# A ninth buffer for half operands in a recurrence, paid for with two shorter rings

## The chip, the cores and the metric

The kernel runs on one core of a Trainium2 chip. The metric is the device time of one execution in microseconds (us), as a median over repeated runs. The core has the engines TensorE (PE in the profile; its weight loads are PEld), VectorE (DVE), ScalarE (ACT), GpSimd (POOL) and SyncE (SP). All of them share 16 DMA engines for transfers between the on-chip memory and DRAM. Transfers issued from SP run on one hardware queue (q1 in the profile), those issued from POOL on a software queue (q0).

## The reference, cut to what matters

The program is one pass of a network with a two-dimensional LSTM, an attention layer and a feed-forward layer that contains a recurrence over time. Only that last recurrence is touched. For 16 images of 4096 tokens with 128 features:

```python
Wx = jnp.einsum('bti,hi->bth', x, W)
Wx = ((flat - mean) * rsqrt(var + eps) * gamma + beta)     # over all B*T rows
Vt = V.T
def step(yt, wx_t):
    yt = jax.nn.sigmoid(wx_t + yt @ Vt)
    return (yt, yt)
_, ys = jax.lax.scan(step, y0, jnp.swapaxes(Wx, 0, 1))      # 4096 steps in order
t = t + swapaxes(ys, 0, 1)
```

## The kernel before

Three stages follow each other: the LSTM, the attention layer for all images, and the recurrence (function `recurrence`, from L1494). The attention stage leaves the products Wx in DRAM (`wx`) and has already written x plus its own result into the output. The recurrence adds its states to that output.

**How the recurrence is tiled.** The 4096 tokens of an image are cut into 128 chunks of 32 (`STEPS`), which are run side by side: each chunk starts from zero, takes 12 warm-up steps (`WARM`) over the last tokens of the chunk before it, and then its own 32 steps (44 in all, `ALL`). A check at the end compares the warmed-up starts with the true ends. Two images (`GI`) form a pair, called a group in the code, and a state `rc_y` of a pair is a tile of 128 features by 2 x 128 columns (1 KB per partition). There are 8 pairs. Four of them are live at a time (`LANES`); the pairs of the first round start at steps 0, 5, 10 and 15 of the common loop, those of the second round at 45, 50, 55 and 60 (`starts`, L1617). The loop has 105 steps.

**One step** of a live pair: PE multiplies the last state by V (`product`, L1587) into PSUM; DVE adds the scaled operand (`state`, L1600); ACT applies the sigmoid (L1608). Every second step of a pair, `turn` (L1569) transposes its two newest states on PE (L1577), and ACT copies the result into a tile `rc_tt` (L1578) that holds four steps (4 KB per partition). When a tile `rc_tt` is full, which takes two such copies two steps apart, POOL issues a DMA that adds it into the output in DRAM (L1581); the DMA reads 512 KB of states and accumulates. So a pair makes 8 such tiles, and the whole recurrence 64. POOL has eight completion semaphores in turn for these DMAs: a store waits for the one eight before it.

**Where the operands lie.** The operand of a pair is cut into two halves by time (`h`): half 1 holds the upper 16 of the 32 tokens of every chunk, half 0 the lower 16. Half 1 is used first (warm-up), from the pair's first step, then half 0 from step 12 to 27, then half 1 again from step 28 to 43. A half takes 16 KB per partition and is loaded by four DMAs from SP of 512 KB each (`load`, L1557, and `half_image`, L1486). There are eight rooms for halves, tags `w0` to `w7`. Rooms 0 to 3 hold the halves of the first two pairs and are loaded during the attention stage (`ahead`, L1748). Rooms 4 to 7 are loaded at the beginning of the recurrence. In the second round the pair in lane l takes over the two rooms of the pair that ran in lane l before: its half 1 goes where the other pair's half 0 was, and its half 0 where the other's half 1 was.

**What sets the order.** PE, DVE, ACT and POOL run in the order in which the loop writes the instructions, with a manual schedule around it. The dictionary `due` (L1618) gives the step at which each load is written into SP's queue. It sets only the order on that queue: SP issues a load as soon as the room's last reader is done and a completion semaphore is free.

**The rings.** States `rc_y` come from a ring of 24 tiles, tiles `rc_tt` from a ring of 10. A tile is reused when its last reader is done; for `rc_tt` that is the DMA of L1581.

Of the kernel before, what the change touches and what calls it, by code (L numbers as in the profile page):

```python
# [8 lines left out]
F32 = mybir.dt.float32  # L9
# [6 lines left out]
P = 128  # L16
# [3 lines left out]
HALF = STEPS // 2  # L20
# [7 lines left out]
def idle_products(nc, out, ident, w, *sizes):  # L28

    for n in sizes:  # L30
        nc.tensor.matmul(out[:, :n], ident, w[:, :n], start=True, stop=True)
# [1462 lines left out]
def recurrence(nc, tc, wx, wx_stats, t2, v, gamma, beta, ident, mhalf, out, early, filler):  # L1494

    B, H = wx.shape[:2]
    N = t2.shape[1]
    L = STEPS
    CH = N // L
    C = 16
    G = CH // C
    S = 4
    NB = L // S
    GI = 2
    LANES = 4  # L1510
    WARM = 12
    AGREE = 2.0 ** -18
    NG = B // GI
    ALL = WARM + L
    APART = 5
    with ExitStack() as ctx:
        cp = ctx.enter_context(tc.tile_pool(name="rc_c", bufs=1))
        vT = cp.tile([P, P], F32, name="rc_vT")
        scale = cp.tile([P, 1], F32, name="rc_scale")
        shift = cp.tile([P, 1], F32, name="rc_shift")  # L1520
        res = cp.tile([P, NG], F32, name="rc_res")
        with ExitStack() as fast:
            wp = fast.enter_context(tc.tile_pool(name="rc_wp", bufs=1))
            yp_ = fast.enter_context(tc.tile_pool(name="rc_yp", bufs=1))
            tp = fast.enter_context(tc.tile_pool(name="rc_tp", bufs=10))
            ps_z = fast.enter_context(tc.tile_pool(name="rc_psz", bufs=4, space=PSUM))
            ps_t = fast.enter_context(tc.tile_pool(name="rc_pst", bufs=4, space=PSUM))

            def fill(*sizes):
                if sizes:  # L1530
                    idle_products(nc, ps_t.tile([P, 512], F32, tag="t", name="rc_t"), ident, filler, *sizes)


            vp = ps_t.tile([P, 4, P], F32, tag="t", name="rc_t")
            nc.tensor.transpose(vp[:, 0, :], v, ident)
            nc.scalar.copy(vT, vp[:, 0, :])
            nc.scalar.activation(shift, mhalf[:, 0:1], AF.Sigmoid)
            fill(*[384] * 8)
            mv = cp.tile([P, 2], F32, name="rc_mv")
            nc.vector.bn_aggr(mv, wx_stats.rearrange("p c s -> p (c s)"))  # L1540
            inv_std(nc, cp, scale, mv[:, 1:2], mhalf, "rc")
            nc.vector.tensor_mul(scale, scale, gamma)
            nc.vector.tensor_mul(shift, mv[:, 0:1], scale)
            nc.vector.tensor_sub(shift, beta, shift)

            class Group:
                pass

            def place(g):
                gr = Group()  # L1550
                gr.g = g
                gr.images = slice(g * GI, (g + 1) * GI)
                gr.w, gr.ys = {}, {}
                gr.last = None
                return gr

            def load(gr, h, n):  # L1557

                k = 2 * (gr.g % LANES) + (1 - h if gr.g < LANES else h)
                if gr.g < LANES and k in early:  # L1560
                    gr.w[h] = early["w", k]
                    return
                if n == 0:
                    pool = early.get(k, wp)
                    gr.w[h] = pool.tile([P, GI, G, HALF, C], F32, tag=f"w{k}", name=f"rc_w{k}")
                i, k = divmod(n, 2)
                half_image(nc, wx, gr.w[h], gr.g * GI + i, h, i, k)

            def turn(gr, s):  # L1569

                k, r = divmod(s, S)
                if r == 0:
                    gr.tt = tp.tile([P, GI, S, H], F32, tag="tt", name="rc_tt")
                yp = ps_t.tile([P, GI, 2, P], F32, tag="t", name="rc_t")
                for i in range(GI):
                    for j in range(2):
                        nc.tensor.transpose(yp[:, i, j, :], gr.ys[s + j][:, i, :], ident)  # L1577
                nc.scalar.copy(gr.tt[:, :, r : r + 2, :], yp)  # L1578
                if r == S - 2:
                    rows = out[gr.images].rearrange("b (c l) f -> c b l f", l=L)[:, :, k * S : (k + 1) * S, :]  # L1580
                    nc.gpsimd.dma_start(out=rows, in_=gr.tt, accum_op=ALU.add)  # L1581

            def product(gr):
                gr.z = None
                if gr.last is not None:
                    gr.z = ps_z.tile([P, GI, CH], F32, tag="z", name="rc_z")
                    nc.tensor.matmul(gr.z, vT, gr.last, start=True, stop=True)  # L1587

            def state(gr, n):


                s = (n - WARM) % L
                w = gr.w[s // HALF][:, :, :, s % HALF, :]
                y = yp_.tile([P, GI, CH], F32, tag="y", name="rc_y", bufs=24)
                yg = y.rearrange("p i (g c) -> p i g c", c=C)
                gr.last = y
                if gr.z is None:
                    nc.scalar.activation(yg, w, AF.Sigmoid, bias=shift, scale=scale)
                    return
                nc.vector.scalar_tensor_tensor(  # L1600
                    yg, w, scale, gr.z.rearrange("p i (g c) -> p i g c", c=C), ALU.mult, ALU.add
                )
                if n == WARM - 1:
                    gr.last = gr.y0 = yp_.tile([P, GI, CH], F32, tag="y0", name="rc_y0", bufs=LANES)
                    nc.vector.memset(gr.y0[:, :, 0:1], 0.0)
                    nc.scalar.activation(gr.y0[:, :, 1:CH], y[:, :, 0 : CH - 1], AF.Sigmoid, bias=shift)
                    return
                nc.scalar.activation(y, y, AF.Sigmoid, bias=shift)  # L1608
                gr.ys[n - WARM] = y

            def check(gr):
                d = yp_.tile([P, GI, CH - 1], F32, tag="d", name="rc_d")
                nc.vector.tensor_sub(d, gr.y0[:, :, 1:CH], gr.last[:, :, 0 : CH - 1])
                nc.vector.tensor_reduce(res[:, gr.g : gr.g + 1], d, AX.XY, ALU.max, apply_absolute_value=True)


            starts = [APART * (g % LANES) + (ALL + 1) * (g // LANES) for g in range(NG)]  # L1617
            due = {  # L1618
                (g, h, n): 0 if g < LANES else starts[g] - (10 if h else 0) + n
                for h in (1, 0) for g in range(NG) for n in range(2 * GI)  # L1620
            }
            groups = {g: place(g) for g in range(NG)}
            with tc.manual_schedule(
                engines={mybir.EngineType.PE, mybir.EngineType.DVE, mybir.EngineType.Activation, mybir.EngineType.Pool}
            ):
                for t in range(max(starts) + ALL + 1):
                    for (g, h, n), at in due.items():
                        if at == t:
                            load(groups[g], h, n)
                    live = [(groups[g], t - starts[g]) for g in range(NG) if 0 <= t - starts[g] <= ALL]  # L1630
                    for gr, n in live:
                        if n < ALL:
                            product(gr)
                    fill(*{1: (384, 256), 2: (384,), 3: (128,)}.get(len(live), ()))
                    for gr, n in live:
                        if n < ALL:
                            state(gr, n)
                    for gr, n in live:
                        s = n - WARM
                        if s > 0 and s % 2 == 0:  # L1640
                            turn(gr, s - 2)
                        if n == ALL:
                            check(gr)

        worst = cp.tile([P, 1], F32, name="rc_worst")
        nc.vector.tensor_reduce(worst, res, AX.X, ALU.max)
        nc.gpsimd.partition_all_reduce(worst, worst, P, bass_isa.ReduceOp.max)
        flag = cp.tile([P, 1], mybir.dt.int32, name="rc_flag")
        nc.vector.tensor_scalar(flag, worst, AGREE, None, ALU.is_gt)
        again = nc.values_load(flag[0:1, 0:1], min_val=0, max_val=1)  # L1650
        with tc.If(again != 0):
            in_order(nc, tc, wx, t2, vT, scale, shift, ident, out)
# [165 lines left out]
```

## Time and profile before

| what | us |
|---|---|
| three runs | 3641.32, 3644.18, 3649.93 (median 3644.18) |
| the profiled execution's own time | 3651.45 |
| its span, first to last instruction | 3649.9 |
| first state of the recurrence (ACT, L1598) | at 3388.16 |
| first store of states issued (POOL, L1581) | at 3420.18 |
| last store issued | at 3639.17 |

Mean busy time of the engines over the whole span: PE 96%, DVE 82%, ACT 68%, POOL 68%. The mean hides the stages. By windows of the recurrence:

| window, us | PE busy | ACT busy | DMA share | granted PE clock |
|---|---|---|---|---|
| 3440 to 3482 (42) | 42.00 | 41.76 | 1.08 | 1.00 |
| 3482 to 3520 (38) | 28.31 | 25.62 | 1.09 | 0.91 |
| 3520 to 3548 (28) | 27.16 | 27.07 | 1.09 | 1.00 |
| 3548 to 3612 (64) | 64.00 | 63.85 | 1.13 | 1.00 |

"DMA share" is the share of time in which the 16 DMA engines had packets under way; about 1 means that they never rest. A line of the waits reads: engine, tile and line that waited, then whom it waited for, then the sum, the number of waits and the longest. A wait for several semaphores is put down to the one that came last by the profile; where the engine named had long been done, it was another, often a DMA. "Landing" is the time from the issue of a DMA to its completion.

### The profile page before, as it was taken

What the parts mean: (1) busy time and instruction counts of PE and PEld (TensorE: products, weight loads), DVE (VectorE), ACT (ScalarE), POOL (GpSimd) and SP (SyncE); (2) the same over time, 40 slices, a digit from 0 to 9 for tenths busy, and PEclk for the clock granted to TensorE, in tenths of its full rate; (3) what the DMA queues carried; (4) which work ended last, traced back from release to release, by engine and by line L of the source; (5) the groups of instructions that cost most, each with busy time, mean ns of one, the idle gap of its engine ahead of it and who ended that gap; (6) DMA issues with size and microseconds to landing.
All of it is one profiled execution on the core that took longest, in us unless ns stands there. A gap on an engine that the chain in (4) does not pass through costs nothing. (4 is left out here: it accounts for less than half of the span.)

```text
span 3649.9 us, 99050 instructions
## 1 busy us (share of the span) xinstructions
PE 3499.9 (96%) x36874; PEld 2368.8 (65%) x36874; DVE 2991.3 (82%) x6997; ACT 2498.5 (68%) x5126; POOL 2484.0 (68%) x3840
## 2 busy tenths in 40 slices
PE   6899999999999998999999999999999999997988
PEld 5666665545567666975666666666666666654777
DVE  7799999998889887534888888888888888888665
ACT  0466566656667665345788888888888888876787
POOL 1577877777788885324777777777777777775123
PEclk9999999999999999999999999999999999999999
DMA  9223232333333221023677666776767677657799
GB/s 320 102 76 80 80 85 80 81 85 84 88 87 85 80 77 35 4 61 96 147 187 188 162 161 161 166 166 161 163 162 165 165 164 165 156 140 189 196 274 183
DMA packets 834182, 484.04 MB, mean 133 GB/s; under 512 B 304672, under 2 KB 800672, under 8 KB 833696
## 3 DMA queue, kind: packets, MB, share of 16 engines
q1 hardware_dynamic: 811034, 441.36, 47.3%
q0 software_dynamic: 17728, 34.61, 5.2%
q8 instruction: 294, 4.82, 0.6%
q10 hardware_dynamic: 4934, 1.68, 0.2%
q14 instruction: 192, 1.57, 0.2%
HBM read 239.21 MB, written 238.29 MB: 131 GB/s over the span
## 5 line engine op out<-in xcount | busy, mean ns | idle before, releaser
L1081 POOL TENSOR_TENSOR at_total<-at_total,at_e 128x512 f32<-128x512 f32 x472 | 601.5, 1274 | 238.4 <-ACT at_e L1054 218.8
L274 ACT ACTIVATE ls_g<-ls_z,ls_b 128x304 f32<-128x304 f32 (+26 forms) x950 | 492.8, 545 | 220.1 <-PE ls_z L272 189.0
L267 PE MATMUL ls_z<-ls_xn,ls_w 128*128 128x432 f32 (+28 forms) x1700 | 586.1, 492 | 1.5 <-POOL ls_xn L259 1.2
L267 PEld LDWEIGHTS ls_z<-ls_xn,ls_w 128*128 128x128 f32 x1700 | 309.4, 190 | 189.0 <-issue 97.8
L272 PE MATMUL ls_z<-ls_hsum,ls_u 128*128 128x304 f32 (+26 forms) x1140 | 366.8, 458 | 0.0
L1013 DVE TENSOR_REDUCE at_mxq<-at_bank 128x1 f32<-128x512 f32 x512 | 317.8, 683 | 55.2 <-PE at_bank L1009 54.9
L307 POOL TENSOR_TENSOR ls_tt<-ls_ve,mhalf 128x8 f32<-128x8 f32 (+2 forms) x190 | 313.0, 1647 | 19.8 <-DVE ls_ve L306 4.2
L1158 ACT ACTIVATE at_eT<-at_bank 128x512 f32<-128x512 f32 x512 | 264.3, 603 | 42.0 <-PE at_bank L1153 41.4
L272 PEld LDWEIGHTS ls_z<-ls_hsum,ls_u 128*128 128x128 f32 x1140 | 208.9, 191 | 128.6 <-issue 78.2
L390 ACT ACTIVATE ls_g<-ls_cell 128x304 f32<-128x304 f32 (+26 forms) x190 | 93.2, 491 | 267.2 <-DVE ls_cell L389 267.1
L272 PE MATMUL ls_z<-ls_h,ls_u 128*128 128x304 f32 (+26 forms) x760 | 254.9, 458 | 11.9 <-DVE ls_h L394 11.9
L324 ACT ACTIVATE ls_tt<-ls_tt,ls_nb 128x128 f32<-128x128 f32 (+9 forms) x632 | 261.0, 478 | 5.5 <-POOL ls_tt L307 5.0
L386 POOL TENSOR_TENSOR ls_g<-ls_g,ls_cell 128x304 f32<-128x304 f32 (+26 forms) x190 | 180.3, 949 | 123.6 <-ACT ls_g L274 110.7
L1124 DVE TENSOR_REDUCE at_cmx<-at_bank 128x8 f32<-128x512 f32 x256 | 175.6, 686 | 103.5 <-PE at_pair L1116 102.0
L259 POOL TENSOR_TENSOR ls_xn<-ls_xn,grstd 128x272 f32<-128x272 f32 (+40 forms) x186 | 209.4, 1126 | 73.6 <-DVE ls_xn L254 70.5
L1229 ACT COPY at_fx<-at_bank 128x512 f32<-128x512 f32 x128 | 133.5, 1043 | 142.3 <-PE at_bank L1225 137.8
L1600 DVE SCALAR_TENSOR_TENSOR rc_y<-rc_w,rc_scale,rc_z 128x256 f32<-128x256 f32 x344 | 154.6, 481 | 86.0 <-PE rc_z L1587 84.2
L1219 ACT ACTIVATE at_z<-at_u,at_nb,at_r 128x128 f32<-128x128 f32 x512 | 209.5, 484 | 4.7 <-POOL at_nb L1214 4.5
L272 PEld LDWEIGHTS ls_z<-ls_h,ls_u 128*128 128x128 f32 x760 | 140.5, 190 | 106.5 <-issue 52.6
L1581 POOL DMA_DIRECT2D out_dram<-rc_tt x64 | 77.4, 1209 | 168.0 <-ACT rc_tt L1578 142.2
L1174 DVE STREAM_TRANSPOSE at_t<-at_bank 128x512 f32<-128x512 f32 x256 | 167.9, 695 | 28.6 <-PE at_bank L1165 27.7
L1587 PE MATMUL rc_z<-rc_y,rc_vT 128*128 128x256 f32 x688 | 173.0, 391 | 12.3 <-ACT rc_y L1608 11.6
(279 smaller groups left out, 9806.1 us busy)
## 6 DMA issues: line engine op xcount, KB each, us to landing
at_win<-vd SPq DMA_DIRECT2D x256, 256.0 KB
t<-ls_tt SPq DMA_DIRECT2D x392, 130.0 KB
at_T<-t SPq DMA_DIRECT2D x128, 264.0 KB
gs_xb<-in_x_dram SPq DMA_DIRECT2D x64, 512.0 KB
at_xh<-t SPq DMA_DIRECT2D x128, 256.0 KB
vd<-at_v SPq DMA_DIRECT2D x128, 256.0 KB
t<-at_u SPq DMA_DIRECT2D x128, 256.0 KB
out_dram<-at_u SPq DMA_DIRECT2D x128, 256.0 KB
```

Of the source, the lines that this page charges most:

```text
L259: eng.tensor_tensor(a, a, norm(v, grstd), ALU.mult)
L267: nc.tensor.matmul(v.z[g][:, : v.total], wt[g], v.xn[:, : v.total], start=True, stop=True)
L272: nc.tensor.matmul(view(v, v.first.z[g]), ut[g], hin, start=False, stop=True, skip_group_check=True)
L274: nc.scalar.activation(a[:, : v.cols], z, AF.Tanh if g == 4 else AF.Sigmoid, bias=bt[g])
L307: nc.gpsimd.tensor_tensor(v.tt[:, 0:k, F + 2 : F + 4], ve[:, :, :k].rearrange("p r k -> p k r"), mhalf[:, : 2 * k].rearrange("p (k r) -> p ...
L324: nc.scalar.activation(v.tt[:q, k, F + 4 :], v.tt[:q, k, 0:F], AF.Identity, bias=v.nb[:q, k : k + 1], scale=v.tt[:q, k, F + 3 : F + 4],)
L386: nc.gpsimd.tensor_mul(v.a[1], v.a[1], v.cl)
L1013: nc.vector.tensor_reduce(gr.im.mxq[:, n : n + 1, gr.g], gr.s[n], AX.X, ALU.max)
L1081: eng.tensor_tensor(total, total, e[:, :, c, :], ALU.add)
L1124: nc.vector.tensor_reduce(gr.mx[:, n : n + k].rearrange("p n c j -> p (n c j)"), s.rearrange("p (x m) -> p x m", m=M), AX.X, ALU.max)
L1158: nc.scalar.activation(gr.eT[:, n], gr.s[n], AF.Exp)
L1219: nc.scalar.activation(gr.z[:, c, :], gr.u[:, c, :], AF.Identity, bias=gr.nb[:, c : c + 1], scale=gr.r3[:, c : c + 1])
```

## The change

A ninth room (`w8`) is added. Its 16 KB per partition come from the rings: states go from 24 to 18 tiles (6 KB less), transposed states from 10 to 8 (8 KB less). The halves of the second round no longer stay in their lane: the list `free` holds each room with the step at which it comes free, beginning with room 8 at step 0, the list `wanted` holds the second round's halves in the order in which they are needed, and the two are paired in order. A load is written into SP's queue at the step at which its room comes free.

The pairing that results, as half of pair: room, step at which the room comes free, step at which the half is needed. Half 1 of pair 4: room 8, 0, 45. Half 1 of pair 5: room 1, 28, 50. Half 1 of pair 6: room 3, 33, 55. Half 0 of pair 4: room 5, 38, 57. Half 1 of pair 7: room 7, 43, 60. Half 0 of pair 5: room 0, 44, 62. Half 0 of pair 6: room 2, 49, 67. Half 0 of pair 7: room 4, 54, 72. Room 6 is not used again.

Before, the same eight halves were written at steps 35 (half 1 of pair 4, room 1), 40 (pair 5, room 3), 45 (pair 6, room 5) and 50 (pair 7, room 7), and 45, 50, 55 and 60 (half 0 of pairs 4 to 7, rooms 0, 2, 4 and 6).

```diff
-            tp = fast.enter_context(tc.tile_pool(name="rc_tp", bufs=10))
+            tp = fast.enter_context(tc.tile_pool(name="rc_tp", bufs=8))
...
             def load(gr, h, n):
-                k = 2 * (gr.g % LANES) + (1 - h if gr.g < LANES else h)
+                k = room[gr.g, h]
...
-                y = yp_.tile([P, GI, CH], F32, tag="y", name="rc_y", bufs=24)
+                y = yp_.tile([P, GI, CH], F32, tag="y", name="rc_y", bufs=18)
...
             starts = [APART * (g % LANES) + (ALL + 1) * (g // LANES) for g in range(NG)]
-            due = {
-                (g, h, n): 0 if g < LANES else starts[g] - (10 if h else 0) + n
-                for h in (1, 0) for g in range(NG) for n in range(2 * GI)
-            }
+            room = {(g, h): 2 * g + 1 - h for g in range(LANES) for h in (1, 0)}
+            free = [(0, 2 * LANES)] + sorted(
+                (starts[g] + WARM + (L if h else HALF), room[g, h]) for g in range(LANES) for h in (1, 0)
+            )
+            wanted = sorted((starts[g] + (0 if h else WARM), g, h) for g in range(LANES, NG) for h in (1, 0))
+            due = {(g, h, n): 0 for h in (1, 0) for g in range(LANES) for n in range(2 * GI)}
+            for (at, k), (_, g, h) in zip(free, wanted):
+                room[g, h] = k
+                due |= {(g, h, n): at + n for n in range(2 * GI)}
```

## The prediction

> **What bounds the kernel now.** The change touches only the recurrence, which by the windows runs from 3388 us to the end of the 3649.9 us span. I read the waits of SyncE, DVE and ScalarE in it first (is any load late?), then the busy time in windows of 10 us (where does it idle?), then the waits and the DMA queues of the idle stretch. The chain that ended last is no help: it holds only the last store.
>
> Who waited for the loaded operands rc_w, in the whole run (us, times):
>
> ```profile
>   DMA rc_w<-wx: 1.4, 1
> ```
>
> Once, 1.4 us, at the first state. No load of the second round is late. Windows (columns: window, length, then busy time and instructions of PE, weight load, DVE, ACT, POOL, then granted clock, DMA share, GB/s):
>
> ```profile
> 3390.00:3400.00 10.00, 9.38 (x32) 5.31 (x31) 2.92 (x7) 3.88 (x8) 0.00 (x0) 1.00 1.02 406
> 3410.00:3420.00 10.00, 9.75 (x49) 7.39 (x49) 7.75 (x18) 9.20 (x20) 0.00 (x0) 1.00 0.00 1
> ...
> 3460.00:3470.00 10.00, 10.00 (x64) 9.03 (x63) 6.69 (x16) 10.00 (x24) 4.53 (x4) 1.00 1.08 291
> ...
> 3500.00:3510.00 10.00, 9.37 (x47) 7.56 (x46) 6.27 (x15) 7.68 (x17) 2.50 (x3) 0.86 1.09 286
> 3510.00:3520.00 10.00, 8.02 (x36) 6.47 (x35) 5.05 (x13) 7.23 (x17) 2.41 (x2) 0.83 1.09 290
> ...
> 3540.00:3550.00 10.00, 10.00 (x55) 8.64 (x55) 8.33 (x20) 9.95 (x24) 2.03 (x2) 1.00 1.10 253
> ```
>
> PE and ACT are full except in one stretch, 3482 to 3520, where ACT is busy 25.62 of 38 us. There the DMA engines are full (share 1.09). The waits of that stretch, 3482 to 3520 (us, times, longest):
>
> ```profile
> POOL out_dram L1581 <- DMA out_dram<-rc_tt: 18.6, 6, 4.1
> PE rc_z L1587 <- ACT rc_y L1608: 9.7, 6, 2.6
> ACT rc_tt L1578 <- DMA out_dram<-rc_tt: 7.3, 4, 2.4
> ACT rc_tt L1578 <- PE rc_t L1577: 3.0, 2, 1.7
> ```
>
> ACT's copy into rc_tt (L1578) waits until an older tile of that ring has been added into the output. The 1.7 us put down to PE is the same wait: those transposes ended 2 us before. So the bound of this stretch is the queue of adding stores, and its slack is the ring. The queues, of 3490 to 3540 and then of 3580 to 3612 (packets, MB, share; issues: count, KB, median us to landing):
>
> ```profile
> q0 software_dynamic: 2992, 5.77, 62.5%
> q1 hardware_dynamic: 2361, 8.56, 45.9%
> out_dram<-rc_tt POOLq DMA_DIRECT2D x12, 512.0 KB, 32.6
> ```
>
> ```profile
> q0 software_dynamic: 3411, 6.57, 112.5%
> out_dram<-rc_tt POOLq DMA_DIRECT2D x14, 512.0 KB, 10.2
> ```
>
> Prices: with stores alone 6.57 MB pass in 32 us, 205 GB/s, so a tile (0.524 MB) takes 2.55 us. With loads alone (first window, 406 GB/s) a load takes 1.29 us. Check on the mixed stretch: 11.0 tiles x 2.55 + 16.3 loads x 1.29 = 28.1 + 21.0 = 49.1 of 50 us. The queues share one capacity, and times add.
>
> **The change, part by part.**
>
> *The ninth room.* Only the order of SyncE's queue changes; PE, DVE, ACT and POOL keep theirs. SyncE does not wait for a step number but for its room's last reader (its waits name DVE rc_y, 117.9 us in 8 waits). So before, groups of four loads start as rooms come free after steps 27, 32, 37, 42, 43, 48, 53 and 58 (the first at 3454.96 by the timeline of SyncE). After, one group goes to the new room at the start, seven start at the same steps 27 to 53 with other contents, and the group after step 58 is gone. What moves is four loads, 4 x 1.29 = 5.2 us of DMA time, from about 3530 to 3540 into 3399 to 3420. There they are hidden by an idle DMA (share 0.00 at 3410 to 3420) and stand behind the loads that the first pairs need; the first store is issued at 3420.18. Were that cover gone they would delay that store 5.2 us, which nobody waits for. At 3530 to 3540 their leaving relieves nobody: ACT runs 9.49 of 10 us there. I take 0, ends -0.5 (that idle half microsecond) and 0. In the last groups two loads of one room stand behind the other's wait for the next step, one step of 2.60 us; with 16 steps or more to go, 0.
>
> *Rooms in the order they come free.* Every half now arrives as early as or earlier than it did. As 1.4 us is all that anybody waited for loads, 0; excluded below zero by the same row.
>
> *States 24 to 18.* Four lanes use four per step, so a state's buffer returns after 4.5 steps. Its last reader is a transpose at most two steps after it was written; on PE that transpose stands ahead of the product that DVE waits for anyway. 0; no other end, because the order of PE, unchanged, excludes a new wait.
>
> *Transposed states 10 to 8.* Full pace is 2.60 us a tile (stores 12 to 16 are issued from 3459.71 to 3470.12). A tile is held 6.3 us before its store is issued (two steps of 2.60 and 1.05 of copies), then until it lands. Ten tiles give 26.0 us for that, hence 19.7 us for landing; eight give 20.8, hence 14.5. The twelfth store, issued at 3459.71, landed when POOL's wait ended at 3480.94: 21.2 us, and at that tile ACT begins to stall. Landing is 5.9 us at the first stores, so it passes 14.5 at about the ninth or tenth, and the stall should begin near 3468 instead of 3482. In this stretch the DMA sets the pace and compute stands at most a ring ahead of it, so compute falls two tiles back. Before, the last stall (ended 3511.75) waited for the 19th tile; after, the same copy waits for the 21st. The DMA must carry two more tiles by then and, if loads follow the steps that free their rooms, the same loads: 2 x 2.55 = 5.1 us. The other end is that the loads are not pushed back: tiles then land every 4.78 us (stores 23 to 28 are issued from 3493.59 to 3517.50), 2 x 4.78 = 9.6. The loads do follow the steps, so I stay at the near end and add 0.9, half of one slow PE chain: the eight product records of the step at 3499.15 take 3.66 us where 1.89 is usual, 1.8 more, after a gap of 2.55 us. More such gaps are coming, mostly under the DMA wait. Together +6.0.
>
> The Trainium skill, "TensorE: Matmul & The Clock Gate" (Part 1: The HAM clock gate), says that the clock halves after an idle window of about 3.4 us. The windows with clock 0.86 and 0.83 had PE gaps of only 2.0 to 2.6 us, so here shorter gaps were enough. By the page no gap would be slow and the sum would stay at 5.1; by the row more will be. The skill, "DMA: Bandwidth & Descriptors" (Anatomy of one DMA), has bytes over 436e3 per us for a transfer; an estimate from it is 1.2 us for a tile, so no queue and no cost at all. The 2.55 us measured decides.
>
> *After the stretch.* The delay is kept: from 3520 on ACT is 9.5 to 10 of 10 us busy, so compute has nothing to catch up with. In the second round the stores land in 10.2 to 11.9 us, under the 14.5 that eight tiles allow, and with four loads fewer ahead of them. 0; if that cover went, see the third rival.
>
> Sum: +6.0 us. The profiled execution is 3651.45 us (span 3649.9 and 1.55 around it) and would be 3657.4. It stood 7.3 above the median shown, 3644.18, which becomes 3650.2.
>
> **Rivals.**
>
> *Faster: the early group drains the queue.* The loads share the DMA that stalls ACT, and 5.2 us of them leave the stretch in which the DMA is full. If the end is set by the DMA's total work, 3644.18 - 5.2 = 3639.0. It decides if any group that competes before 3520 is the one that goes. Against it: the one that goes starts after step 58, behind the stall.
>
> *No cost: absorbed.* At the hand-over no store is issued from 3539.62 to 3547.95, and the DMA's backlog drains. If compute has slack there, a gain or loss below 1 us: 3645. Against it: ACT at 9.95 of 10 in that window.
>
> *Worse: the second round stalls too, or the clock stays low.* The margin there is 14.5 - 11.9 = 2.6 us. If landing grows past 14.5 by 2 us, each of the last three turns of the ring pays 2: +6 on +6.0, 3656; with three more slow chains of 1.8 under no cover, +5.4, 3661.6. For it: DMA share 1.13 through that round. Against it: landing falls there.
>
> **How the numbers follow.** A measurement can tell about 0.2%, 7.3 us. The ring's price (+5.1 to +9.6, forecast 3650.2, its own range 3649 to 3654) has 0.60. Runs shown lie 8.6 us apart, so I split it 0.32 below 7.3 us and 0.28 above. Faster rival 0.14, of which 0.02 falls within 0.2%; absorbed 0.09; worse 0.17. Faster 0.12, same 0.32 + 0.09 + 0.02 = 0.43, slower 0.28 + 0.17 = 0.45. The range leaves out the faster rival and the far end of the worst: 3642 to 3660.
>
> **What would show it.** Right: POOL's waits for rc_tt stores vanish (18.6 us now), since ACT's wait comes first; ACT's idle time at L1578 begins near 3468 and grows by about 5 us; the longest landing falls from 36 to about 30; four loads lie at 3399 to 3405; step for step the second round lies 5 to 6 us later; landing there is under 11 us. Wrong: ACT stalls begin no earlier; a DVE wait for rc_w appears; the second round shows stalls at L1578; or the stretch to 3520 shortens.

## The result, and the profile after

The change makes the kernel slightly slower. The ratio of after to before is 1.0018, with a 95% interval of 1.0012 to 1.0024; the medians of 22 runs each are 3654.24 and 3649.66 us. The forecast was +6.0 us; the medians differ by 4.6, the ratio is worth 6.6 us, its interval 4.4 to 8.8. The absolute forecast, 3650.2 us, was built on the median of the three runs shown, 3644.18; over 22 runs the kernel before has 3649.66, so the measured 3654.24 lies 4.0 above that forecast, though inside its range of 3642 to 3660.

The runs of one kernel scatter over 12 to 16 us, and the profiled execution of the changed kernel was already 1.9 us later when the recurrence began. So the executions are compared from the first state of the recurrence (ACT, L1598: 3388.2 before, 3390.1 after). From there to the end of the span it took 261.7 us before and 265.0 after: 3.3 us more.

Windows of the profile after (columns as in the prediction: window, length, busy time and instructions of PE, weight load, DVE, ACT, POOL, granted clock, DMA share, GB/s):

```profile
3400.00:3410.00 10.00, 9.60 (x35) 5.42 (x35) 5.20 (x11) 5.71 (x12) 0.00 (x0) 1.00 1.03 411
...
3467.00:3482.00 15.00, 12.40 (x75) 10.45 (x73) 8.20 (x19) 10.24 (x25) 4.82 (x4) 1.00 1.09 281
...
3548.00:3612.00 64.00, 64.00 (x387) 57.44 (x386) 46.35 (x107) 64.00 (x149) 25.16 (x21) 1.00 1.07 186
```

The ninth room's loads follow those of the first pairs and end by about 3414 (351 GB/s from 3410 to 3415, 6 from 3415 to 3420). That is later than the forecast's 3399 to 3405, but ahead of the first store at 3422.09, which comes 32.0 us after the first state in both profiles. From 3467 to 3482, where ACT was busy for 14.76 of 15 us before, it now works 10.24. The second round is again full (64 of 64 us), and its stores no longer press: 186 GB/s instead of 206.

The waits of the profile after, from 3420 to 3548 (us, times, longest):

```profile
POOL out_dram L1581 <- ACT rc_tt L1578: 116.0, 32, 32.7
ACT rc_tt L1578 <- DMA out_dram<-rc_tt: 12.6, 8, 3.0
ACT rc_tt L1578 <- PE rc_t L1577: 3.1, 2, 1.8
POOL out_dram L1581 <- DMA out_dram<-rc_tt: 0.9, 1, 0.9
```

ACT's wait for a free tile of the ring has grown from 7.3 + 3.0 us to 12.6 + 3.1. POOL's own wait for the eighth store back has all but gone, from 18.6 to 0.9: with eight tiles ACT is stopped before POOL is. The first of these stalls on ACT and the last long one, in the timeline before:

```profile
3484.37 1.07 ACT L1578 COPY rc_tt<-rc_t 128x512 f32<-128x512 f32 x2 [1.71 <-PE rc_t L1577]
...
3511.75 0.58 ACT L1578 COPY rc_tt<-rc_t 128x512 f32<-128x512 f32 x1 [1.73 <-DMA out_dram<-rc_tt]
```

and after:

```profile
3472.76 0.59 ACT L1578 COPY rc_tt<-rc_t 128x512 f32<-128x512 f32 x1 [1.04 <-DMA out_dram<-rc_tt]
...
3518.25 0.59 ACT L1578 COPY rc_tt<-rc_t 128x512 f32<-128x512 f32 x1 [3.02 <-DMA out_dram<-rc_tt]
```

The first begins at 3471.7, which is 81.6 us after the first state; before it was 3482.7, or 94.5 us. The last long one ends 128.2 us after the first state; before, the same copy, the 56th of that line, came at 3511.75, or 123.6. It is 4.6 us late. (After it the ring makes ACT wait once more, 0.55 us at 3527.31.)

**Where the 4.6 us come from.** The DMA queues, from 3430 to the end of that last stall, before (3511.7):

```profile
q0 software_dynamic: 5060, 9.77, 67.5%
q1 hardware_dynamic: 3057, 11.15, 37.1%
```

and after (3431.9 to 3518.25):

```profile
q0 software_dynamic: 5553, 10.72, 69.5%
q1 hardware_dynamic: 3061, 11.17, 35.3%
```

Up to the same copy the same loads have passed (11.15 and 11.17 MB), and 0.95 MB more of stores: 1.8 tiles. At 2.55 us a tile, the price taken from the second round, that is 4.6 us. This is the sum of the prediction, found in the bytes. In tt8_only below, the same count (3426.9 to 3513.6) gives 10.86 MB of stores and 10.96 of loads: 2.1 tiles more and 0.4 loads less than before, 4.8 us, for a stall that ends 4.9 us later.

### The profile page after: what moved, and what is told of

Same layout as the page of the kernel before. It is cut to its first block, busy times and chain, and to the rows that moved or that the text cites. A ratio compares the mean times of both kernels' runs of the same rounds, so it can differ in the third digit from the quotient of the medians.

```text
span 3655.1 us, 99039 instructions
## 1 busy us (share of the span) xinstructions
PE 3507.4 (96%) x36874; PEld 2373.0 (65%) x36874; DVE 2992.3 (82%) x6997; ACT 2500.2 (68%) x5126; POOL 2484.5 (68%) x3840
## 5 line engine op out<-in xcount | busy, mean ns | idle before, releaser
L390 ACT ACTIVATE ls_g<-ls_cell 128x304 f32<-128x304 f32 (+26 forms) x190 | 93.2, 491 | 266.4 <-DVE ls_cell L389 266.3
L272 PE MATMUL ls_z<-ls_h,ls_u 128*128 128x304 f32 (+26 forms) x760 | 255.8, 459 | 11.9 <-DVE ls_h L394 11.9
```

Source lines behind the costliest of these rows:

```text
L272: nc.tensor.matmul(view(v, v.first.z[g]), ut[g], hin, start=False, stop=True, skip_group_check=True)
```

## The experiments

In all of them "from the first state" means from the first L1598 of that profile (its line number moves by some lines in edited kernels). Three positions tell the kernels apart: the start of the last pair, the issue of the last store, and the end of the span.

| kernel | ratio to before (95%) | last pair starts | last store | end |
|---|---|---|---|---|
| before | 1 | 148.2 | 251.0 | 261.7 |
| the change | 1.0018 (1.0012 to 1.0024) | 151.6 | 254.6 | 265.0 |
| tt8_only | 1.0011 (1.0002 to 1.0020) | 153.1 | 255.8 | 266.4 |
| room9_tt10 | 0.9997 (0.9988 to 1.0006) | 147.1 | 249.7 | 260.3 |
| tt13_y12 | 0.9989 (0.9980 to 0.9998) | 134.2 | 237.9 | 257.6 |
| loads_twice | 1.0018 (1.0009 to 1.0027) | 147.8 | 254.2 | 267.9 |
| tt6_only | 1.0041 (1.0029 to 1.0054) | 159.1 | 261.6 | 272.3 |
| tt13_skip4 | 0.9978 (0.9967 to 0.9988) | 134.2 | 235.5 | 251.8 |
| no_reload | 0.9960 (0.9945 to 0.9974) | 134.2 | 237.3 | 248.1 |
| s8_tt7 | 1.0017 (1.0008 to 1.0026) | 135.9 | 255.8 | 269.4 |
| s2_tt26_y12 | 1.0005 (0.9993 to 1.0017) | 140.5 | 255.0 | 264.7 |
| s2_room9_tt20 | 0.9997 (0.9985 to 1.0008) | 146.9 | 252.0 | 261.5 |

The theory under test is that the shorter ring of transposed states is the whole cost and the ninth room is worth nothing here. The rivals are that the room gives something back, that the 18 states or the new order cost something, and that the stores fall behind by themselves.

### tt8_only: the shorter ring alone

```diff
-            tp = fast.enter_context(tc.tile_pool(name="rc_tp", bufs=10))
+            tp = fast.enter_context(tc.tile_pool(name="rc_tp", bufs=8))
```

> The kernel before with one edit: the ring of transposed states rc_tt from 10 to 8. Eight rooms in the old order, 24 states. Theory A (the shorter ring of rc_tt is the whole cost, the ninth room is worth nothing): ratio to before 1.001 to 1.002 (+3.5 to +7 us), the first ACT stall at L1578 near 3468 us instead of 3482 on the clock of the profile before, and the last one ends about 5 us later. Rival B (the ninth room gives back part of what the ring costs): clearly slower than the change, +8 to +12 us. Rival C (the cost is in the order of the rooms or in the 18 states): no difference to before.

The ratio is 1.0011 and the last pair starts 4.8 us late; ACT waits at L1578 for 15.2 us up to there. The first stall begins 79.1 us after the first state, which is 3467.2 on the clock of the profile before (3468 expected). The last one ends 128.5 us after the first state, 4.9 us later than before:

```profile
3513.62 0.58 ACT L1578 COPY rc_tt<-rc_t 128x512 f32<-128x512 f32 x1 [2.84 <-DMA out_dram<-rc_tt]
```

So one number in the kernel before makes the cost of the change. The room gives nothing back that can be seen: the two intervals overlap, and the change ends only 1.3 us earlier in these two profiles. For 1.1 us of that, a slow stretch of PE is the likelier cause, as argued at the end of the next experiment.

### room9_tt10: the ninth room without the shorter ring

```diff
-            tp = fast.enter_context(tc.tile_pool(name="rc_tp", bufs=8))
+            tp = fast.enter_context(tc.tile_pool(name="rc_tp", bufs=10))
...
-                y = yp_.tile([P, GI, CH], F32, tag="y", name="rc_y", bufs=18)
+                y = yp_.tile([P, GI, CH], F32, tag="y", name="rc_y", bufs=12)
```

(against the changed kernel)

> The change with rc_tt kept at 10; the memory for the ninth room comes from the states alone (24 to 12). Theory A: no difference to before, within 0.1% (-0.5 to +1 us), stalls at the same tiles for the same time. Rival B (the ninth room takes 5 us of loads out of the full stretch): 3 to 5 us faster than before. Rival C (shorter ring of states costs): slower, with new DVE waits at L1600 for PE transposes L1577.

No difference: 0.9997, with 1 inside the interval. Pairs 4 and 5 start at 107.0 and 125.5, where the kernel before has 106.6 and 125.3. The stalls are nearly those of before. The first wait for the ring, 0.6 us, begins at 92.1, where the kernel before has 0.24 us put down to PE; all together take 11.5 us instead of 10.3; and the last long one ends at 123.8 instead of 123.6. So the room, the order of the rooms and a ring of states cut to half, taken together, neither cost nor gain anything that can be measured. The last pair starts 1.1 us earlier than before, and this difference too arises behind the last long stall.

**A slow stretch of PE, present or absent.** The profiles have the same work between the start of pair 5 and that of pair 6, behind the last long stall; the ring takes 0.5 us there in the change and in room9_tt10, and nothing in the other two. This work takes 12.2 us before, 12.1 in tt8_only, 11.0 in the change and 10.9 in room9_tt10. In the windows of 5 us around it the granted clock is 0.80 and 0.86 before and 0.70 in tt8_only, and 1.00 in the other two. tt6_only and loads_twice below agree: 12.2 us each, with windows of 0.66 and 0.73. On PE, the eight products behind the last long stall, before:

```profile
3512.80 3.65 PE L1587 MATMUL rc_z<-rc_y,rc_vT 128*128 128x256 f32 x8 [1.99 <-ACT rc_y L1608]
```

in tt8_only:

```profile
3514.67 3.62 PE L1587 MATMUL rc_z<-rc_y,rc_vT 128*128 128x256 f32 x8 [3.10 <-ACT rc_y L1608]
```

and in the change, with two earlier groups:

```profile
3482.87 3.35 PE L1587 MATMUL rc_z<-rc_y,rc_vT 128*128 128x256 f32 x8 [2.23 <-ACT rc_y L1608]
3503.93 3.61 PE L1587 MATMUL rc_z<-rc_y,rc_vT 128*128 128x256 f32 x8 [2.56 <-ACT rc_y L1608]
...
3519.30 1.99 PE L1587 MATMUL rc_z<-rc_y,rc_vT 128*128 128x256 f32 x8 [3.27 <-ACT rc_y L1608]
```

Eight products take 1.9 to 2.0 us at a clock of 1.00 and up to 3.7 in a slow stretch. The slow groups of the four profiles began after gaps of PE of 2.0 to 3.1 us, but not every such gap is followed by one: the gap of 3.27 us in the change is not, nor one of 2.18 us before (at 3494.17). The change has two slow groups like the kernel before, but both lie ahead of its last long stall. There a later wait for the ring can absorb them, and no cost of theirs shows: that stall is late by the 4.6 us of the stores alone. The second slow group of the kernel before lies behind the last stall. So 1.2 us of the difference between the change and the kernel before, and 1.1 of that to tt8_only, go with whether the last stall ends in a slow stretch. I did not force one, so this rests on the agreement of six profiles.

### tt6_only: a larger dose

```diff
-            tp = fast.enter_context(tc.tile_pool(name="rc_tp", bufs=10))
+            tp = fast.enter_context(tc.tile_pool(name="rc_tp", bufs=6))
```

> The kernel before with the ring rc_tt at 6 instead of 10. Theory A (two tiles less of lead cost one fixed amount, paid once in the first round): twice what 8 cost there, so pair 7 starts about 9 to 10 us later after the recurrence's start than before, and the second round has no stall at L1578, because a shorter ring also keeps the store queue short (6 x 2.60 - 6.3 = 9.3 us for a landing that is 6 to 8 us with a short queue); ratio 1.002 to 1.003. Rival (landing in the second round is 10 us by nature): ACT stalls at L1578 through the second round too, 1 us and more per turn of the ring, ratio 1.004 and more.

The last pair starts 10.8 us late, a little more than twice the 4.8 us of tt8_only, and from there to the last store it is 102.6 us, as before (102.8): the second round does not stall (the last wait at L1578 for a store ends at 134.4, ahead of the start of pair 5). The rival of a second round that stalls falls; the longest landing is 22.2 us here against 36.0, and the median 9.2 against 12.0, because a short ring also keeps the queue short. The ratio of 1.0041 (10.6 to 19.7 us) is more than the expected 1.002 to 1.003; the profile's 10.6 us lies at its lower end. By the ratio alone the rival would have stood; it is the profile that rules it out.

### tt13_y12: the opposite trade

```diff
-            tp = fast.enter_context(tc.tile_pool(name="rc_tp", bufs=10))
+            tp = fast.enter_context(tc.tile_pool(name="rc_tp", bufs=13))
...
-                y = yp_.tile([P, GI, CH], F32, tag="y", name="rc_y", bufs=24)
+                y = yp_.tile([P, GI, CH], F32, tag="y", name="rc_y", bufs=12)
```

> The opposite trade: eight rooms in the old order, states 24 to 12, and the 12 KB go to rc_tt, 10 to 13. Theory A: three tiles more of lead, so the last ACT stall should all but vanish: at 4.78 us a tile in the crowded stretch or 2.55 us a tile in the ledger, 3 tiles are 7.7 to 14 us, capped by the 12 us for which ACT is idle in the stretch: 7 to 12 us faster than before (ratio 0.9967 to 0.998), ACT waits at L1578 for DMA below 2 us. Then POOL's wait for the eighth store back is what remains, and nobody waits for POOL. Rival (the stall comes from the eight stores that may be in flight, not from the ring): no gain, ACT keeps waiting.

The stalls are gone, with 0.3 us left at L1578, and the last store is issued 13.1 us earlier. But the run gains only 0.1% (0.02 to 0.20%), 4.1 us in the profile. The windows of its end show where the rest stayed:

```profile
3620.00:3630.00 10.00, 2.90 (x14) 1.96 (x12) 1.64 (x5) 1.59 (x3) 2.12 (x3) 0.79 1.13 206
3630.00:3640.00 10.00, 0.00 (x0) 0.00 (x0) 0.00 (x0) 0.00 (x0) 0.00 (x0) 0.50 1.13 203
3640.00:3650.00 10.00, 0.00 (x0) 0.00 (x0) 0.00 (x0) 0.00 (x0) 0.00 (x0) 0.56 0.09 17
```

All computing is done by 3627, and the DMA engines go on at 203 to 206 GB/s until about 3641. The bound has moved from the ring to the total work of the DMA. My expectation had the cap at the idle time of ACT and forgot this one.

### tt13_skip4: what the ninth room would be worth then

```diff
                 k = 2 * (gr.g % LANES) + (1 - h if gr.g < LANES else h)
+                if gr.g == NG - 1 and h == 0:
+                    gr.w[h] = groups[LANES - 1].w[1]
+                    return
```

(added to tt13_y12, ahead of the line on k; the last pair's half 0 is not loaded)

> tt13_y12 with the last four loads left out (half 0 of the last pair is not loaded; the pair reads the half that lies in room 6 already, so its states are not those of the reference). Theory: with 13 tiles the end is set by the DMA's total work, so 4 x 1.29 = 5.2 us less of it end the run about 5 us earlier than tt13_y12: the last landing moves, the computing does not. That is what the ninth room would be worth in such a kernel. Rival (the end of tt13_y12 is set by the latency of its last stores): no difference to tt13_y12.

It ends 251.8 us after the first state, 5.8 earlier than tt13_y12, while all pairs start within 0.1 us of the same times. (The last store is issued 2.4 us earlier too, since POOL waits 1.4 us instead of 5.1 for the eighth store back.) With a long ring, 5 us of loads taken out of the crowded time are worth about 5 us. The ninth room should do this too, but no run shows it together with a ring of 13. Counted from the tile sizes, rooms, states and transposed tiles take 192 KB per partition before, 194 after the change (the two rings give 14 of the 16 KB that the room takes) and 196 in room9_tt10, the most of any run here; nine rooms, 12 states and 13 tiles would take 208.

### no_reload: stores without loads beside them

```diff
+                if gr.g >= LANES:
+                    gr.w[h] = groups[gr.g - LANES].w[h]
+                    return
                 k = 2 * (gr.g % LANES) + (1 - h if gr.g < LANES else h)
```

> The kernel before without any load for the second round: pairs 4 to 7 read the halves that pairs 0 to 3 left in their rooms (the states of the second round are not those of the reference). Rings as before, 10 and 24. Theory A (stores alone, at 2.55 us a tile, keep up with 2.60 us of computing; it is the loads' turns at the DMA engines that make them fall behind): no ACT stall at L1578 in the first round, landing below 15 us throughout, last store issued about 12 to 13 us earlier after the recurrence's start, run 10 to 13 us faster (ratio 0.9965 to 0.997). Rival (the stores fall behind by themselves): stalls remain at about the same tiles.

With the old ring of ten the stalls are gone but for 0.5 us at the very end (3630.11): the pairs start to a tenth of a microsecond where they do in tt13_y12. (That one has 12 states and this one 24, so cutting the states costs nothing here either.) The landing, before and then in no_reload:

```profile
DMA to landing us min/median/max: 5.8/12.0/36.0
```

```profile
DMA to landing us min/median/max: 5.6/6.8/9.4
```

So the stores do not fall behind by themselves; it takes the loads beside them. One window of the first round:

```profile
3490.00:3500.00 10.00, 10.00 (x66) 9.09 (x65) 7.12 (x17) 10.00 (x24) 4.84 (x5) 1.00 1.12 196
```

The DMA share is 1.12 here too, although the stores land in 9.4 us or less. A share of 1 and more is no proof of a queue; the landing is.

### loads_twice: more loads beside the stores

```diff
-                half_image(nc, wx, gr.w[h], gr.g * GI + i, h, i, k)
+                for _ in range(2 if gr.g in (LANES, LANES + 1) and h else 1):
+                    half_image(nc, wx, gr.w[h], gr.g * GI + i, h, i, k)
```

> The kernel before, with the four loads of half 1 of pairs 4 and 5 (rooms that come free after steps 27 and 32) issued twice over, the same data into the same place: eight more loads of 1.29 us before the last stall ends. Theory A (stores and loads share one capacity and times add): the last stall ends up to 8 x 1.29 = 10.3 us later, and the run takes 7 to 10 us more than before, with ACT waiting at L1578. Rival (the stores are limited by themselves, by their own latency or by the ring, and loads pass beside them): less than 2 us more.

The run takes 0.18% longer, but not in the way that I expected. The stalls of the first round are as before (the last pair starts at 147.8 against 148.2). From 3430 to the end of the last stall 9.67 MB of stores and 11.12 MB of loads passed, as in the kernel before (9.77 and 11.15): the extra loads did not push in between, they only stood in line (28 loads were issued in that time instead of 24). SP's queue waited 88.8 us for its own loads; a repeat waits until the load that it overwrites has landed. The cost came later: DVE waited 3.0 us for an operand, and the DMA finished late, 13.7 us after the last store was issued instead of 10.7. So the 10.3 us of extra transfers cost 6.2 us at the end of the profile, but nothing within the crowded stretch. There the two queues take turns packet by packet while both have work: from 3515 to 3545 the stores moved 1605 packets and the loads 1606.

### s8_tt7, s2_tt26_y12 and s2_room9_tt20: another size of tile

The edit in each is `S = 4` to 8 or 2 in `recurrence`, with the ring's size in the same memory: 7 tiles of 8 KB, 26 of 2 KB (both with 12 states, eight rooms), and in the third 20 of 2 KB on the changed kernel with 12 states.

> tt13_y12 with tiles of eight steps instead of four (S from 4 to 8, 1 MB each, seven of them): half as many adding stores, with runs of 4 KB instead of 2 KB in the output. If the store's price is set by bytes (205 GB/s with stores alone), the DMA's total stays and the run ends like tt13_y12, perhaps 1 to 3 us later for the larger last tile and the coarser lead. If it is set by the 2 KB runs, GB/s with stores alone rises clearly above 207 and the run ends up to 10 us earlier than tt13_y12.

The rate with stores alone is 206 GB/s in the mean (3600 to 3640; 194 to 211 by windows of 10 us), so runs of 4 KB are no cheaper than runs of 2 KB. It is slower than tt13_y12 by more than I said: the last store is 17.9 us later, and DVE waits 16.5 us for rc_w (1.4 in the kernel before). The computing is not ahead of tt13_y12 (pair 5 starts at 113.6 against 112.9); it is the loads that come slower. The two queues (packets, MB, share) while both have work, in tt13_y12 from 3488 to 3530:

```profile
q0 software_dynamic: 2245, 4.33, 55.6%
q1 hardware_dynamic: 2247, 8.16, 52.1%
```

in s8_tt7 from 3490 to 3530:

```profile
q0 software_dynamic: 1455, 5.58, 69.8%
q1 hardware_dynamic: 1454, 5.30, 35.5%
```

and in s2_tt26_y12 from 3483 to 3513:

```profile
q1 hardware_dynamic: 2106, 7.66, 68.4%
q0 software_dynamic: 2103, 2.03, 42.0%
```

Each queue moves as many packets as the other, so the size of the store's packets decides how the bytes are shared. With runs of 4, 2 and 1 KB the stores get 140, 103 and 68 GB/s, and the loads 132, 194 and 255.

> tt13_y12 with tiles of two steps instead of four (S from 4 to 2, 256 KB each, 26 of them in the same 52 KB): every copy is stored at once. If the store's price stays at 205 GB/s with runs of 1 KB, the DMA starts about 4 us earlier (two steps) with the same total, and the run ends about 4 us earlier than tt13_y12, 8 us earlier than before. If runs of 1 KB cost more, GB/s with stores alone falls below 200 and the end, set by the DMA, moves back: at 150 GB/s by some 50 us.

Runs of 1 KB pass at 196 GB/s, 5% dearer, neither of my two cases. And beside loads the stores now get only 68 GB/s, as the rows above show, while eight stores in flight are half as many bytes: POOL waits for the eighth store back, 10.7 us, and ACT for a tile behind it, 6.4 us. No run separates these two causes. No gain over the kernel before.

> The change with tiles of two steps, 20 of them (40 KB, as 10 of the old ones) and 12 states. A tile is now held about 1 us instead of 6.3 before its store is issued, so 20 half tiles at 1.30 us leave 25 us for landing, as 12 old tiles would. If 1 KB runs cost no more per byte: hardly a stall, and the ninth room takes its 5.2 us from a DMA that now sets the end, so this is the fastest, 8 to 12 us below before (ratio 0.997 to 0.998). If they cost more, it falls behind like s2_tt26_y12, by 5 us less.

It equals the kernel before (0.9997), so the hope of 8 to 12 us was wrong. The same reasons: 196 GB/s with stores alone, 0.67 MB of stores against 2.54 of loads from 3485 to 3495, and POOL's limit of eight (16.1 us), with ACT waiting 10.7 us for a tile behind it.

## Why the prediction was right or wrong

- **The bound** (the store queue sets the pace of one stretch, its slack is the ring): right. no_reload and tt13_y12 remove the stall (0.5 and 0.3 us are left) from both ends, by taking the loads away and by a longer ring, to the same start times.
- **The ninth room and the order of rooms at 0**: right, by room9_tt10 (0.9997, with the 18 states cut further to 12). No wait for rc_w is left in the profile after.
- **States 24 to 18 at 0**: right, even at 12.
- **Transposed states at +5.1, with 9.6 as the other end**: the mechanism and the size are right. 4.6 us at the last stall in the change and 4.9 in tt8_only. The argument that loads follow the steps, which put it at the near end, is in the bytes: the same 11.2 MB of loads, 1.8 tiles more of stores.
- **Start of the stall near 3468**: 3471.7, or 3469.8 on the clock of the profile before.
- **+0.9 for half a slow PE chain**: the wrong sign. Both kernels have two slow groups, but both of the change lie ahead of its last long stall, where no cost of theirs shows, while the second of the kernel before lies behind it; 1.2 us were made up so. That is also why the step "the delay is kept" fell short: 4.6 us at the last stall, 3.4 at the start of the last pair, 3.3 at the end. In tt8_only, which has a slow group behind its last stall like the kernel before, the delay was kept (4.9, 4.8, 4.6).
- **The sum of +6.0**: near the ratio's 6.6 us, but in part by luck. In the profiles the terms come to 4.6 - 1.2, that is 3.3 at the end.
- **Rivals.** Absorbed: only those 1.2 us, and not by slack. Second round stalls: no, and tt6_only shows why the rule of the allowed landing was incomplete: the landing falls with the ring. Faster by the DMA's total work: not in this kernel, but right in kind in one with a longer ring (tt13_skip4).
- **Signs to look for.** POOL's waits vanished (18.6 to 0.9), the longest landing fell from 36.0 to 30.8, the four loads lie behind those of the first pairs, up to about 3414, landing in the second round is 7.7 us in the median (3548 to 3630; 10.5 before). The second round is 3.4 us later, not 5 to 6.
- **What stays open.** The ratio says 4.4 to 8.8 us, the profile 3.3 after the first state and 1.9 before it. The work before the recurrence is the same, and single executions scatter by more than that: in the twelve profiles the first state lies between 3381.4 and 3399.1. I could not tell whether a microsecond or two of the ratio lies there. What decides whether a PE gap is followed by a slow stretch was not tested either.

The rule of the Trainium skill on the clock ("TensorE: Matmul & The Clock Gate", Part 1) speaks of an idle window of about 3.4 us; here slow stretches came after gaps of 2.0 to 3.1 us and were absent after one of 3.27 us.

## What to carry to other kernels

Before memory moves from one ring to another, find out which ring is the slack of the busiest queue. Here, in a stretch where transfers set the pace, every buffer less cost its own transfer time once (2.3 to 2.7 us a tile), and a prefetch that nobody waited for repaid nothing. A longer ring pays only until the next bound, here the total work of the DMA; the two changes would have to go together, 208 KB by the count above, and no run tried that. If one of them is to be had, it is the opposite of this change: 12 states, 13 transposed tiles and eight rooms (tt13_y12) are the fastest version found that leaves nothing out, 0.9989 of the time before.

## What the runs showed of the hardware that was not expected

- With stores alone, adding stores pass at 205 to 207 GB/s with runs of 2 KB, 206 with 4 KB and 196 with 1 KB; plain loads reach 406 to 411. An adding store costs about twice a load of the same size (2.55 against 1.29 us); no run separates the adding from the other queue and the other direction.
- While both queues have work, they move equal numbers of packets (2245 and 2247, 1455 and 1454, 2103 and 2106), so longer runs in the stores take bytes from the loads: 194 GB/s of loads beside runs of 2 KB, 132 beside 4 KB.
- More loads waiting in the load queue (28 issued instead of 24) took nothing from the store queue beside it (9.67 MB against 9.77 in the same stretch).
- A DMA share of 1.12 can go with a landing of 6.8 us in the median (no_reload) as well as with one of 10 and more.
- In a slow stretch of PE eight products take up to 3.7 us instead of 1.9 to 2.0. Where nothing else waits, profiles with one are about 1.2 us longer than those without; ahead of a wait for the DMA no cost shows.
